# The first product of layer 0's experts as three one-pass products, and its neighbours' loads and tables moved

## The chip, the cores and the metric

The program runs on one core of a Trainium2 chip. Its engines are named as in the profile: PE (TensorE, matmuls), PEld (the weight loads that go with them), DVE (VectorE), ACT (ScalarE), POOL (GpSimd) and SP (SyncE, which here issues DMAs). The metric is the device time of one execution in microseconds (us); lower is better. The kernel before the change takes 3702.06 us, the median of three runs (3697.73 to 3706.18).

## The reference, cut to what matters

Two transformer layers run over 2048 tokens of width 512. Each layer is an attention followed by a mixture of experts. The change is in the mixture of layer 0, which is:

```python
probs = jax.nn.softmax(xr @ Wg, axis=-1)            # 2048 tokens, 8 experts
gate_vals, expert_idx = jax.lax.top_k(probs, 2)
...                                                 # each expert takes at most 640 tokens
dispatched = xr[dispatch_mask.reshape(-1) % S].reshape(E, C, d)      # 8 x 640 x 512
h = jax.nn.relu(jnp.einsum('ecd,edf->ecf', dispatched, w1))          # w1: 8 x 512 x 2048
expert_out = jnp.einsum('ecf,efd->ecd', h, w2)                       # w2: 8 x 2048 x 512
...
out = jnp.einsum('ks,ksm->sm', combine_weights, rerouted)
```

Everything is float32. After it come layer 1's attention, which needs rotation tables (sines and cosines of the positions times two norm vectors) and four weight matrices Wq, Wk, Wv, Wo, and then layer 1's experts.

## The kernel before, in words

Layer 0's attention, layer 0's experts, layer 1's attention and layer 1's experts follow each other. The experts of layer 0 are the class `Experts0` (L1225), called by `layer0_experts` (L1380).

An expert's 640 places are five blocks of 128. The first four are always computed (`FULL` = 4, so 512 places); the fifth is computed only where the expert has tokens there, inside `tc.If(self.used[e])` in `last` (L1318). The inner width 2048 is cut into 16 slices of 128. For each of the 8 x 16 = 128 pairs of expert e and slice k, which are called steps here, `run` (L1352) records:

- `first(e, k)` (L1300): the first product into the PSUM bank `h`. It is four matmuls in `inner` (L1284), one for each 128 of the input width, with a 128x128 piece of w1 as weight and 512 columns of `xT` moving. A float32 matmul stands in the trace as two records. ACT's Relu reads the bank and writes `hT`.
- `second` of the step before (L1309): four matmuls, one for each block, into the banks `o0` to `o3`, which add up over the 16 slices. After the last slice `result` (L1340) scales them by the gate (ACT and DVE in turn) and POOL scatters them with an adding DMA into `x_dram`.
- at each fourth step `last`, the fifth block of a group of four slices (banks `hl` and `ol`), where it is used.
- at the even steps, for the next expert: `fetch` (L1273), POOL's gathering DMA of a block of token rows, and `turn` (L1278), four transposes on PE into the bank `tr` (`transpose4`) and a copy by DVE into `xT`.
- at the steps 4 to 13 of an expert one call of `extra`: first the 16 batches of `rope_tables` (L1170), one per step, then ten loads of 1 MB for layer 1's attention (Wk, Wv, four parts of Wq, four of Wo).

The eight PSUM banks are `h`, `tr`, `o0` to `o3`, `hl`, `ol`, one buffer each. The weights w1 and w2 come in units of two slices by SP's DMAs (`weights0`, L1216), with four and six buffers. PE, DVE, ACT and POOL take their instructions in the order of the recording (`Engines`, L74, keeps it); SP's DMAs and the bodies of the If are placed by the framework's scheduler.

A rotation batch (`batch`, L1185) runs on DVE, ACT (Sin, Abs, Sin), DVE again and then nine small multiplications on POOL, into one buffer `rp_r`, from which SP writes the table to HBM.

After the last expert, `kept.close()` frees the expert weights and `layer1_attention` (L1634) begins: SP loads the token rows `xn` from `x_dram`, and PE starts with the products of the context rows, which need Wk and Wv.

Of the kernel before, what the change touches and what calls it, by code (L numbers as in the profile page):

```python
# [11 lines left out]
F32 = mybir.dt.float32  # L12
BF16 = mybir.dt.bfloat16
I32 = mybir.dt.int32
U32 = mybir.dt.uint32
U16 = mybir.dt.uint16
F32R = mybir.dt.float32r
AF = mybir.ActivationFunctionType
ALU = mybir.AluOpType
# [4 lines left out]
P = 128  # L24
NB = 16
D = 512
NC = D // P
NH = 16
G0 = 8
G1 = 4  # L30
E = 8
SPAN = NB * P
CAP = 640
# [9 lines left out]
FW1 = NC * 2 * FF1  # L43
FW = FW1 + 3 * D
FP8_MAX = 448.0
SCALE = float(np.float32(1.0 / np.sqrt(128.0)))
TWO_PI = float(2.0 * np.pi)
TWO_PI_A = 6.28125
# [34 lines left out]
class Ops:  # L83
# [34 lines left out]
    def t(self, pool, shape, dt, tag, bufs=None):  # L118
        self.uid += 1
        return pool.tile(shape, dt, name=f"{tag}_{self.uid}", tag=tag, bufs=bufs)  # L120
# [59 lines left out]
class Routing:  # L180
# [22 lines left out]
    def turn(self):  # L203
        self.ps = self.r.ops.transpose4(self.psum, self.xn)
# [1011 lines left out]
def weights0(ops, args, pool, e, f):  # L1216

    w1 = ops.t(pool, [P, NC, 256], F32, "w1", KEPT_UNITS["w1"])
    ops.nc.sync.dma_start(out=w1, in_=args["f0_w1"][e, f])
    w2 = ops.t(pool, [P, 2, D], F32, "w2", KEPT_UNITS["w2"])  # L1220
    ops.nc.sync.dma_start(out=w2, in_=args["f0_w2"][e, f])
    return w1, w2


class Experts0:  # L1225
# [7 lines left out]

    SLICES = FF0 // P
    GROUP = 4
    FULL = NBLK0 - 1

    def __init__(  # L1240
        self, ops, tc, args, router, x_dram, sum_dram, small, work, psum, kept_pool, zero, begun
    ):
        self.plain, self.tc = ops.nc, tc
        ops.nc = Engines(tc, ops.nc)
        self.ops, self.args, self.work, self.psum = ops, args, work, psum
        self.kept_pool, self.zero = kept_pool, zero[0:1]
        self.x_dram, self.sum_dram = x_dram, sum_dram
        self.table = router.table
        self.source, self.target = slot_rows(ops, small, self.table[:, :P], P, SPAN // P)

        self.views = dram_disjoint_views(sum_dram, NBLK0)
        self.mark = sum_dram[SUMS - 1 :, :]
        self.xT, self.g, self.h, self.rest, self.outs = {}, {}, {}, {}, {}
        self.w = begun
        self.h_last = ops.t(psum, [P, self.GROUP, P], F32, "hl")
        self.o_last = ops.t(psum, [P, D], F32, "ol")
        ops.nc.vector.memset(self.h_last, 0.0)
        ops.nc.vector.memset(self.o_last, 0.0)

        used = ops.t(small, [P, E], I32, "used")  # L1260
        last = self.table[:, :P].rearrange("p (e b) -> p e b", e=E)[:, :, self.FULL]
        ops.nc.vector.tensor_scalar(used, last, 0.0, None, ALU.is_gt)
        loads, self.used = self.plain.values_load_multi_w_load_instructions(
            used[0:1, :], engines=(mybir.EngineType.PE,), min_val=0, max_val=1,
            skip_runtime_bounds_check_because="it is the result of a comparison",
        )
        for i in loads:
            tc.keep_in_program_order(i)
# [7 lines left out]
        gather(self.ops, g, self.x_dram, self.source[:, col : col + 1])  # L1276

    def turn(self, e, b):  # L1278
        if b == 0:
            self.xT[e] = self.ops.t(self.work, [P, NC, CAP], F32, "xT", 2)  # L1280
        ps = self.ops.transpose4(self.psum, self.g.pop((e, b)))
        self.ops.nc.vector.tensor_copy(self.xT[e][:, :, b * P : (b + 1) * P], ps)

    def inner(self, ps, e, k, s):  # L1284

        w1, at = self.w[e, k // 2][0], k % 2 * P
        for c in range(NC):
            self.ops.nc.tensor.matmul(
                ps, w1[:, c, at : at + P], self.xT[e][:, c, s],
                start=(c == 0), stop=(c == NC - 1),  # L1290
            )

# [5 lines left out]
        )  # L1298

    def first(self, e, k):  # L1300
        n = self.FULL * P
        if k % 2 == 0 and (e, k // 2) not in self.w:
            self.w[e, k // 2] = weights0(self.ops, self.args, self.kept_pool, e, k // 2)
        ps = self.ops.t(self.psum, [P, n], F32, "h")
        self.inner(ps, e, k, slice(0, n))
        hT = self.h[e, k] = self.ops.t(self.work, [P, n], F32, "hT", 4)
        self.ops.nc.scalar.activation(hT, ps, AF.Relu)

    def second(self, e, *slices):  # L1309
        if slices[0] == 0:  # L1310
# [7 lines left out]
    def last(self, e, group, before):  # L1318


        g = self.GROUP
        with self.tc.If(self.used[e]):  # L1322
            if before is not None:
                for i in range(g):
                    self.outer(self.o_last, e, before * g + i, self.rest[e, before][:, i, :])
            if group is not None:
                for i in range(g):
                    s = slice(self.FULL * P, CAP)
                    self.inner(self.h_last[:, i, :], e, group * g + i, s)
        if group is not None:  # L1330
            rest = self.rest[e, group] = self.ops.t(self.work, [P, g, P], F32, "rest", 2)
            self.ops.nc.vector.tensor_scalar(rest, self.h_last, 0.0, None, ALU.max)
        else:
            self.result(e, self.FULL, self.o_last)

            self.ops.nc.sync.dma_start(
                out=self.mark.rearrange("p (a c) -> p a c", a=4), in_=self.zero
            )
# [10 lines left out]
            nc.scalar.activation(y, out, AF.Copy, scale=weight)  # L1349
        scatter_add(self.ops, self.views[b], self.target[:, col : col + 1], y)  # L1350

    def run(self, extra):  # L1352
        for b in range(NBLK0):
            self.fetch(0, b)
            self.turn(0, b)
        groups = self.SLICES // self.GROUP
        steps = [(e, k) for e in range(E) for k in range(self.SLICES)]
        for i, (e, k) in enumerate(steps):
            self.first(e, k)
            if 0 < i < len(steps) - 1:  # L1360
                self.second(*steps[i - 1])
            group, at = divmod(k, self.GROUP)
            if at == self.GROUP - 1:
                self.last(e, group, group - 1 if group else None)
            if e and k == 0:
                self.last(e - 1, None, groups - 1)
            if e + 1 < E and k % 2 == 0:
                b = k // 2 - 2
                if 0 <= b + 2 < NBLK0:
                    self.fetch(e + 1, b + 2)  # L1370
                if 0 <= b < NBLK0:
                    self.turn(e + 1, b)
            if 4 <= k < 14 and extra:
                extra.pop(0)()
        self.second(E - 1, self.SLICES - 2, self.SLICES - 1)
        self.last(E - 1, None, groups - 1)
        self.ops.nc = self.plain


def layer0_experts(ops, tc, args, router, x_dram, sum_dram, small, kept_pool, zero, begun, extra):  # L1380
    with ExitStack() as ctx:
        work = ctx.enter_context(tc.tile_pool(name="b_work", bufs=1))
        psum = ctx.enter_context(tc.tile_pool(name="b_ps", bufs=1, space=PSUM))
        job = Experts0(
            ops, tc, args, router, x_dram, sum_dram, small, work, psum, kept_pool, zero, begun
        )
        job.run(extra(work))

# [466 lines left out]
def xattn_moe_two_layers(ctx: ExitStack, tc: tile.TileContext, args, out):  # L1857
    nc = tc.nc
    const = ctx.enter_context(tc.tile_pool(name="const", bufs=1))
    dram = ctx.enter_context(tc.tile_pool(name="dram", bufs=1, space=DRAM))  # L1860
    ops = Ops(nc, tc, const)
    t = ops.t
# [5 lines left out]
    nw = t(const, [P, 2 * P], F32, "nw")  # L1868
    nc.sync.dma_start(out=nw, in_=args["norms"])
    x0_dram = t(dram, [SPAN, D], F32, "x0_dram")  # L1870
    x1_dram = t(dram, [SPAN, D], F32, "x1_dram")

    x_dram = t(dram, [SUMS, D], F32, "x_dram")
# [10 lines left out]
    begun = {}  # L1884
    zero = []
# [8 lines left out]
    }  # L1894
    layer0_attention(ops, tc, args, x_rows, vec, router0, kept_pool, ahead)

    with tc.tile_pool(name="c_w", bufs=1) as wpool:
        wq = t(wpool, [P, NC, NH * P], F32, "c_wq")
        wk = t(wpool, [P, NC, D], F32, "c_wk")
        wv = t(wpool, [P, NC, D], F32, "c_wv")  # L1900
        wo = t(wpool, [P, NH, D], F32, "c_wo")

        def ahead(work):

            loads = [(wk, args["Wk"]), (wv, args["Wv"])]
            for c in range(4):
                s = slice(c * D, (c + 1) * D)
                loads.append((wq[:, :, s], args["Wq"][:, :, s]))
            for c in range(4):
                h = slice(4 * c, 4 * c + 4)  # L1910
                loads.append((wo[:, h, :], args["Wo"][:, h, :]))
            calls = rope_tables(ops, args, work, nw, rope_dram)

            def load(to, source):

                ops.nc.vector.memset(to[:, 0:1, 0:1], 0.0)
                nc.sync.dma_start(out=to, in_=source)

            return calls + [lambda a=a: load(*a) for a in loads]

        layer0_experts(
            ops, tc, args, router0, x0_dram, x_dram, wpool, kept_pool, zero[0], begun, ahead
        )
        kept.close()
        layer1_attention(
            ops, tc, args, x_rows, (wq, wk, wv, wo), rope_dram, router1, out, wpool
        )
    layer1_experts(ops, tc, args, router1, x1_dram, out)

# [71 lines left out]
```

## Time and profile before

| what | us |
|---|---|
| median of three runs | 3702.06 |
| the profiled execution's own time | 3698.0 |
| its span, first to last instruction | 3696.2 |
| stage of layer 0's attention | 0 to 1277 |
| stage of layer 0's experts | 1277 to 2298 |
| stage of layer 1's attention | 2298 to about 3336 |
| stage of layer 1's experts | to the end |

The stages are read from the first and last starts of the groups. A line of the groups gives line, engine, operation, output tile and input tiles, shapes, count, then busy time, mean duration of one, and the idle time before them with what ended it. L69 is the line of the helper through which every recorded instruction goes, so groups are told apart by their tiles. A matmul's duration in its record has a tail that overlaps the next one; the time between two starts is what a matmul costs in a row of them. A line of the timeline gives start, time, engine, operation, tiles, count, and in brackets the idle time before it.

### The profile page before, as it was taken

The numbers are of one execution on the slowest core, as the hardware profiler recorded it, in microseconds if no ns is written. First come the engines' busy times: TensorE is split into PE (matmuls) and PEld (weight loads), VectorE is DVE, ScalarE is ACT, GpSimd is POOL, SyncE is SP. The second block draws the span as 40 slices with busy tenths as digits, with TensorE's granted clock in tenths as the row PEclk, the third lists the DMA queues.
The fourth block names the chain that finished last, engine by engine and source line by source line (L and its number), as shares of the span: only waits on it lengthen the run. The fifth ranks groups of instructions, "written<-read, shape, count | busy, mean of one in ns | idle before, by whom it ended". The sixth has DMA issues, their size and how long they took to land. (4 is left out here: it accounts for less than half of the span.)

```text
span 3696.2 us, 42676 instructions
## 1 busy us (share of the span) xinstructions
PE 3532.1 (96%) x13220; PEld 2111.1 (57%) x13220; DVE 1756.6 (48%) x4203; ACT 1500.5 (41%) x5601; POOL 1265.6 (34%) x1596
## 2 busy tenths in 40 slices
PE   6899999999999699999999999899999999997998
PEld 3666666788888444444444454455555555554655
DVE  6888899877688521100000000445555555553111
ACT  5777677788877111101100101443444343441111
POOL 6566677654244222101110100423333333321332
PEclk8999999999999799999999999999999999998999
DMA  4556755744523133453332331000001010006333
GB/s 159 167 175 205 260 199 194 275 147 145 177 90 122 52 115 98 135 167 100 105 91 63 104 76 25 31 23 30 27 22 35 22 32 19 21 12 236 69 63 55
DMA packets 156777, 382.80 MB, mean 104 GB/s; under 512 B 18080, under 2 KB 21312, under 8 KB 154752
## 3 DMA queue, kind: packets, MB, share of 16 engines
q1 hardware_dynamic: 138848, 338.49, 27.3%
q0 software_dynamic: 17696, 41.43, 5.9%
q8 instruction: 119, 1.95, 0.2%
q14 instruction: 114, 0.93, 0.1%
HBM read 266.32 MB, written 113.52 MB: 103 GB/s over the span
## 5 line engine op out<-in xcount | busy, mean ns | idle before, releaser
L69 PE MATMUL h<-xT,w 128*128 128x512 f32 x1024 | 467.2, 594 | 4.0 <-PEq L1322 1.1
L69 PE MATMUL o<-w,hT 128*128 128x512 f32 x1024 | 460.8, 592 | 0.0
L69 ACT ACTIVATE hT<-h 128x512 f32<-128x512 f32 x128 | 76.3, 596 | 852.8 <-PE h L69 852.8
L69 PEld LDWEIGHTS o<-w,hT 128*128 128x128 f32 x1024 | 194.2, 190 | 243.7 <-issue 243.0
L69 DVE COPY xT<-tr 128x512 f32<-128x512 f32 x79 | 54.4, 688 | 572.4 <-PE tr L69 572.4
L69 PEld LDWEIGHTS h<-xT,w 128*128 128x128 f32 x1024 | 189.6, 190 | 231.0 <-issue 229.3
L69 ACT ACTIVATE p<-sc,sm_nm 128x128 f32<-128x128 f32 (+1 forms) x768 | 302.7, 420 | 20.9 <-PE tr L69 10.4
L69 PE MATMUL mm<-w,xq 128*128 128x512 f32 x1024 | 275.8, 411 | 5.5 <-DVE xq L69 4.0
L69 PE MATMUL sc<-kT,qT 128*128 128x128 f32 (+1 forms) x1536 | 267.4, 310 | 4.7 <-ACT qT L69 4.4
L69 ACT ACTIVATE hn_sq<-mm 128x128 f32<-128x128 f32 x768 | 214.8, 280 | 128.1 <-PE mm L69 105.4
L69 POOL DMA_INDIRECT x_dram<-y,e_target x40 | 62.6, 1564 | 572.0 <-ACT y L69 562.3
L69 PE MATMUL pv<-pT,v 128*128 128x256 f32 (+1 forms) x768 | 255.8, 456 | 1.4 <-ACT pT L69 1.4
L69 PEld LDWEIGHTS sc<-kT,qT 128*128 128x128 f32 x1536 | 222.4, 191 | 46.0 <-issue 29.7
L69 PE MATMUL mm<-c_wq,hT 128*128 128x512 f32 x512 | 231.4, 595 | 0.7 <-DVE qn L69 0.7
L69 PE MATMUL po<-c_wo,oT 128*128 128x512 f32 x512 | 231.4, 595 | 0.0
L69 DVE TENSOR_REDUCE sm_nm<-sc 128x4 f32<-128x512 f32 (+1 forms) x256 | 175.5, 685 | 92.1 <-PE sc L69 92.0
L69 PE MATMUL po<-w,cq 128*128 128x512 f32 x512 | 192.4, 457 | 24.8 <-DVE cq L69 3.4
L69 POOL TENSOR_TENSOR hn_rs<-hn_rs,mhalf 128x4 f32<-128x4 f32 x192 | 205.2, 1069 | 16.0
L69 PEld LDWEIGHTS mm<-w,xq 128*128 128x128 f32 x1024 | 185.4, 191 | 43.6 <-DVE xq L69 4.8
L69 ACT ACTIVATE rms_sq<-mm 128x128 f32<-128x128 f32 x384 | 106.8, 278 | 251.5 <-PE mm L69 230.8
L69 PE MATMUL h<-e_w,xT 128*128 (+1 forms) x624 | 200.5, 465 | 4.3 <-DMA e_w<-in_f_w 3.5
L69 PE MATMUL mm<-w,xk 128*128 128x512 f32 x512 | 187.3, 508 | 0.9 <-POOL w L69 0.8
(248 smaller groups left out, 6388.6 us busy)
## 6 DMA issues: line engine op xcount, KB each, us to landing
w<-in_f_w SPq DMA_DIRECT2D x128, 512.0 KB, 3.7
kept_w<-st SPq DMA_DIRECT2D x66, 512.0 KB, 2.9
w<-kept_w SPq DMA_DIRECT2D x66, 512.0 KB, 5.6
x_dram<-xr SPq DMA_DIRECT2D x64, 256.0 KB, 2.0
xr<-x_dram SPq DMA_DIRECT2D x64, 256.0 KB, 2.8
e_w<-in_f_w SPq DMA_DIRECT2D x8, 1408.0 KB
xk<-in_ctxT SPq DMA_DIRECT2D x32, 256.0 KB, 3.8
xv<-in_ctxT SPq DMA_DIRECT2D x32, 256.0 KB, 3.0
```

The lines of the kernel that those rows point to most:

```text
L69: return self.tc.keep_in_program_order(call(*args, **kwargs))
```

## The change

The first product of the four full blocks is no longer a float32 matmul. Both operands are cut into an upper part `hi`, whose lowest 12 bits are zero, and the exact rest. With w = hi + lo for the weights and x likewise, and S = `SPLIT` = 4096, three matmuls of type float32r are made for each 128 of the input width: hi_w by hi_x and lo_w by S lo_x, added in the bank `h`, and (hi_w - S lo_w) by (hi_x - S lo_x) in the bank `tr`. The result is (1 + 1/S) times the first sum less 1/S times the second.

- `cut`, `split` (new): three DVE instructions and one ACT instruction of 128x512 make the three parts of a slice of w1, one step ahead of their use, with two buffers for each part.
- `turn`: ACT copies the transposed block out of `tr`, then DVE (three instructions) and ACT (two more) make the parts of x. The fifth block is kept whole (`x_last`), copied by DVE.
- `first`: 12 one-pass matmuls in place of 4 float32 ones; then ACT scales the second bank (`less`), DVE combines it with the first (`hT`), and ACT's Relu works in place in SBUF.
- `extra` is called at the even steps from 4 on (4, 6, ... 14): 16 rotation batches, then the loads of Wk and Wv, so that they end in the third expert.
- The space for the parts of x is taken from where Wq and Wo lay. Wq is loaded at step 2 of the last expert, when the pool `b_even` is closed; Wo after the last expert, when the pool of expert weights is closed, in four DMAs of 1 MB that stand ahead of layer 1's first loads of token rows in SP's order.

The second product, the fifth block and all that comes before and after are unchanged.

```diff
     def turn(self, e, b):
...
+        ps = self.ops.transpose4(self.psum, self.g.pop((e, b)))
+        if b == self.FULL:
+            x = self.x_last[e] = t(work, [P, NC, P], F32, "x_last", 2)
+            nc.vector.tensor_copy(x, ps)
+            return
...
+        upper, lower, part = (x[:, :, b * P : (b + 1) * P] for x in self.x[e])
+        raw = t(work, [P, NC, P], F32, "x_raw", 2)
+        nc.scalar.copy(raw, ps)
+        hi = self.cut(raw, [P, NC, P], "x_hi")
+        nc.scalar.copy(upper, hi)
+        nc.vector.tensor_tensor(raw, raw, hi, ALU.subtract)
+        nc.scalar.activation(lower, raw, AF.Copy, scale=SPLIT)
+        nc.vector.scalar_tensor_tensor(part, raw, -SPLIT, hi, ALU.mult, ALU.add)
+
+    def cut(self, raw, shape, tag):
+
+        hi = self.ops.t(self.work, shape, F32, tag, 2)
+        self.ops.nc.vector.tensor_scalar(
+            hi.bitcast(U32), raw.bitcast(U32), 12, 12, ALU.logical_shift_right,
+            ALU.logical_shift_left,
+        )
+        return hi
+
+    def split(self, e, k):
...
+        hi = self.cut(raw, [P, NC, P], "w_hi")
+        nc.scalar.copy(upper, hi)
+        nc.vector.tensor_tensor(lower, raw, hi, ALU.subtract)
+        nc.vector.scalar_tensor_tensor(part, lower.bitcast(F32), -SPLIT, hi, ALU.mult, ALU.add)
+        self.split_w[e, k] = upper, lower, part
...
     def first(self, e, k):
-        ps = self.ops.t(self.psum, [P, n], F32, "h")
-        self.inner(ps, e, k, slice(0, n))
-        hT = self.h[e, k] = self.ops.t(self.work, [P, n], F32, "hT", 4)
-        self.ops.nc.scalar.activation(hT, ps, AF.Relu)
+        upper, lower, part = self.split_w.pop((e, k))
+        x_upper, x_lower, x_part = self.x[e]
+        rest = t(self.psum, [P, n], F32, "h")
+        for i, (w, x) in enumerate(((upper, x_upper), (lower, x_lower))):
+            for c in range(NC):
+                nc.tensor.matmul(
+                    rest, w[:, c, :], x[:, c, :],
+                    start=(i == 0 and c == 0), stop=(i == 1 and c == NC - 1),
+                )
+
+        parts = t(self.psum, [P, n], F32, "tr")
+        for c in range(NC):
+            nc.tensor.matmul(
+                parts, part[:, c, :], x_part[:, c, :], start=(c == 0), stop=(c == NC - 1)
+            )
+        hT = self.h[e, k] = t(self.work, [P, n], F32, "hT", 4)
+        less = t(self.work, [P, n], F32, "less", 2)
+        nc.scalar.activation(less, parts, AF.Copy, scale=-1.0 / SPLIT)
+        nc.vector.scalar_tensor_tensor(hT, rest, 1.0 + 1.0 / SPLIT, less, ALU.mult, ALU.add)
+        nc.scalar.activation(hT, hT, AF.Relu)
...
         for i, (e, k) in enumerate(steps):
+            if i + 1 < len(steps):
+                self.split(*steps[i + 1])
             self.first(e, k)
...
-            if 4 <= k < 14 and extra:
+            if k >= 4 and k % 2 == 0 and extra:
                 extra.pop(0)()
+            if (e, k) == (E - 1, 2):
+                late()
```

More of the change, by code (lines that the diff above doesn't have):

```diff
@@ L45 @@
 FP8_MAX = 448.0
+SPLIT = 4096.0
 SCALE = float(np.float32(1.0 / np.sqrt(128.0)))
@@ L1240, in __init__ @@
     def __init__(
-        self, ops, tc, args, router, x_dram, sum_dram, small, work, psum, kept_pool, zero, begun
+        self, ops, tc, args, router, x_dram, sum_dram, small, work, psum, kept_pool, zero, begun,
+        even_pool,
     ):
@@ L1245, in __init__ @@
         self.ops, self.args, self.work, self.psum = ops, args, work, psum
-        self.kept_pool, self.zero = kept_pool, zero[0:1]
+        self.kept_pool, self.zero, self.even_pool = kept_pool, zero[0:1], even_pool
         self.x_dram, self.sum_dram = x_dram, sum_dram
@@ L1252, in __init__ @@
         self.mark = sum_dram[SUMS - 1 :, :]
-        self.xT, self.g, self.h, self.rest, self.outs = {}, {}, {}, {}, {}
+        self.x, self.x_last, self.g, self.h, self.rest, self.outs = {}, {}, {}, {}, {}, {}
+        self.split_w = {}
         self.w = begun
@@ L1278, in turn, with inner @@
     def turn(self, e, b):
-        if b == 0:
[L1280 to L1284, printed above, removed]
+        nc, t, work = self.ops.nc, self.ops.t, self.work
+        ps = self.ops.transpose4(self.psum, self.g.pop((e, b)))
[3 more added lines that the diff above has]
+            return
+        if b == 0:
+            pool = work if e % 2 else self.even_pool
+            self.x[e] = [t(pool, [P, NC, self.FULL * P], F32R, f"x{i}") for i in range(3)]
+        upper, lower, part = (x[:, :, b * P : (b + 1) * P] for x in self.x[e])
[14 more added lines that the diff above has]
+    def split(self, e, k):
+        nc, t = self.ops.nc, self.ops.t
+        if k % 2 == 0 and (e, k // 2) not in self.w:
+            self.w[e, k // 2] = weights0(self.ops, self.args, self.kept_pool, e, k // 2)
+        raw = self.w[e, k // 2][0][:, :, k % 2 * P : (k % 2 + 1) * P]
+        upper, lower, part = (
+            t(self.work, [P, NC, P], F32R, f"w{i}", 2) for i in range(3)
+        )
[4 more added lines that the diff above has]
+        self.split_w[e, k] = upper, lower, part
+    def inner(self, ps, e, k):
         w1, at = self.w[e, k // 2][0], k % 2 * P
@@ L1288, in inner @@
             self.ops.nc.tensor.matmul(
-                ps, w1[:, c, at : at + P], self.xT[e][:, c, s],
+                ps, w1[:, c, at : at + P], self.x_last[e][:, c, :],
                 start=(c == 0), stop=(c == NC - 1),
@@ L1300, in first @@
     def first(self, e, k):
-        n = self.FULL * P
-        if k % 2 == 0 and (e, k // 2) not in self.w:
-            self.w[e, k // 2] = weights0(self.ops, self.args, self.kept_pool, e, k // 2)
-        ps = self.ops.t(self.psum, [P, n], F32, "h")
-        self.inner(ps, e, k, slice(0, n))
-        hT = self.h[e, k] = self.ops.t(self.work, [P, n], F32, "hT", 4)
-        self.ops.nc.scalar.activation(hT, ps, AF.Relu)
+        nc, t, n = self.ops.nc, self.ops.t, self.FULL * P
+        upper, lower, part = self.split_w.pop((e, k))
[11 more added lines that the diff above has]
+                parts, part[:, c, :], x_part[:, c, :], start=(c == 0), stop=(c == NC - 1)
+            )
+        hT = self.h[e, k] = t(self.work, [P, n], F32, "hT", 4)
[3 more added lines that the diff above has]
+        nc.scalar.activation(hT, hT, AF.Relu)
     def second(self, e, *slices):
@@ L1327, in last @@
                 for i in range(g):
-                    s = slice(self.FULL * P, CAP)
-                    self.inner(self.h_last[:, i, :], e, group * g + i, s)
+                    self.inner(self.h_last[:, i, :], e, group * g + i)
         if group is not None:
@@ L1350, in result, with run @@
         scatter_add(self.ops, self.views[b], self.target[:, col : col + 1], y)
-    def run(self, extra):
+    def run(self, extra, late):
+        self.split(0, 0)
         for b in range(NBLK0):
@@ L1377, in run, with layer0_experts, last_expert @@
         self.ops.nc = self.plain
-def layer0_experts(ops, tc, args, router, x_dram, sum_dram, small, kept_pool, zero, begun, extra):
-    with ExitStack() as ctx:
-        work = ctx.enter_context(tc.tile_pool(name="b_work", bufs=1))
+def layer0_experts(
+    ops, tc, args, router, x_dram, sum_dram, small, kept_pool, zero, begun, extra, late
+):
+    with ExitStack() as ctx, ExitStack() as even:
+        even_pool = even.enter_context(tc.tile_pool(name="b_even", bufs=1))
+        work = ctx.enter_context(tc.tile_pool(name="b_work", bufs=1, side="right"))
         psum = ctx.enter_context(tc.tile_pool(name="b_ps", bufs=1, space=PSUM))
         job = Experts0(
-            ops, tc, args, router, x_dram, sum_dram, small, work, psum, kept_pool, zero, begun
-        )
-        job.run(extra(work))
+            ops, tc, args, router, x_dram, sum_dram, small, work, psum, kept_pool, zero, begun,
+            even_pool,
+        )
+        def last_expert():
+            even.close()
+            late()
+        job.run(extra(even_pool), last_expert)
 ORDER1 = (
@@ L1895, in xattn_moe_two_layers, with load @@
     layer0_attention(ops, tc, args, x_rows, vec, router0, kept_pool, ahead)
-    with tc.tile_pool(name="c_w", bufs=1) as wpool:
-        wq = t(wpool, [P, NC, NH * P], F32, "c_wq")
+    with ExitStack() as attention1:
+        wpool = attention1.enter_context(tc.tile_pool(name="c_w", bufs=1))
         wk = t(wpool, [P, NC, D], F32, "c_wk")
         wv = t(wpool, [P, NC, D], F32, "c_wv")
-        wo = t(wpool, [P, NH, D], F32, "c_wo")
+        late = []
+        def load(to, source):
+            ops.nc.vector.memset(to[:, 0:1, 0:1], 0.0)
+            nc.sync.dma_start(out=to, in_=source)
@@ L1903, in ahead @@
         def ahead(work):
-            loads = [(wk, args["Wk"]), (wv, args["Wv"])]
-            for c in range(4):
[L1907 to L1917, printed above, removed]
@@ L1919, in ahead, with large @@
-            return calls + [lambda a=a: load(*a) for a in loads]
+            calls = rope_tables(ops, args, work, nw, rope_dram)
+            return calls + [lambda: load(wk, args["Wk"]), lambda: load(wv, args["Wv"])]
+        def large(name, shape, count, source):
+            pool = attention1.enter_context(tc.tile_pool(name=name, bufs=1))
+            w = t(pool, shape, F32, name)
+            for c in range(4):
+                s = slice(c * count, (c + 1) * count)
+                part = (slice(None), slice(None), s) if name == "c_wq" else (slice(None), s)
+                nc.sync.dma_start(out=w[part], in_=source[part])
+            late.append(w)
@@ L1921, in xattn_moe_two_layers @@
         layer0_experts(
-            ops, tc, args, router0, x0_dram, x_dram, wpool, kept_pool, zero[0], begun, ahead
+            ops, tc, args, router0, x0_dram, x_dram, wpool, kept_pool, zero[0], begun, ahead,
+            lambda: large("c_wq", [P, NC, NH * P], D, args["Wq"]),
         )
         kept.close()
+        large("c_wo", [P, NH, D], 4, args["Wo"])
         layer1_attention(
-            ops, tc, args, x_rows, (wq, wk, wv, wo), rope_dram, router1, out, wpool
+            ops, tc, args, x_rows, (late[0], wk, wv, late[1]), rope_dram, router1, out, wpool
```

## The prediction

> **What bounds the kernel now.** I read the busy time by stage first, then the groups, then the timeline. In the stage of layer 0's experts:
>
> ```profile
> core 0: us, PE busy (x) PEld busy (x) DVE busy (x) ACT busy (x) POOL busy (x), PEclk, DMA share, GB/s
> 1277.00:2298.00 1021.00, 1014.29 (x2831) 483.59 (x2830) 100.76 (x286) 105.66 (x201) 132.67 (x215) 1.00 0.34 97
> ```
>
> PE is busy for 1014 of 1021 us at full clock; DVE and ACT work for a tenth of it. So PE's work is the stage's time, and work put on DVE and ACT is free as long as PE never waits for it. Whose work that is, from the groups:
>
> ```profile
> L69 PE MATMUL h<-xT,w 128*128 128x512 f32 x1024 | 467.2, 594 | 4.0 <-PEq L1322 1.1
> L69 PE MATMUL o<-w,hT 128*128 128x512 f32 x1024 | 460.8, 592 | 0.0
> L69 ACT ACTIVATE hT<-h 128x512 f32<-128x512 f32 x128 | 76.3, 596 | 852.8 <-PE h L69 852.8
> L69 DVE COPY xT<-tr 128x512 f32<-128x512 f32 x79 | 54.4, 688 | 572.4 <-PE tr L69 572.4
> L69 PE MATMUL mm<-w,xq 128*128 128x512 f32 x1024 | 275.8, 411 | 5.5 <-DVE xq L69 4.0
> ```
>
> The first product (`h`) and the second (`o`) share the stage. Only `h` changes. What one costs is the time between starts:
>
> ```profile
> 1801.48 3.60 PE L69 MATMUL h<-xT,w 128*128 128x512 f32 x8
> 1804.91 3.60 PE L69 MATMUL o<-w,hT 128*128 128x512 f32 x8
> 1805.17 0.60 ACT L69 ACTIVATE hT<-h 128x512 f32<-128x512 f32 x1 [6.27 <-PE h L69]
> ```
>
> `o` starts 3.43 us after `h`: 8 records of 0.429. A step is 6.86 us, 128 steps 878 us; the rest is the fifth block and transposes. ACT starts 0.26 us after the stream ended.
>
> **The gain.** The price of a one-pass float32r record is in layer 0's attention, where `mm<-w,xq` is such a product (64 block passes x 2 x 8 matmuls = 1024 records, one each):
>
> ```profile
> 690.72 0.60 PE L69 MATMUL tr<-ident,kn 128*128 128x128 f32 x4
> 691.08 2.12 PE L69 MATMUL mm<-w,xq 128*128 128x512 f32 x8
> 693.04 0.59 PE L69 MATMUL pv<-pT,v 128*128 128x256 f32 x2
> ```
>
> The last transpose starts at 691.05 and costs 0.109; so eight records run from 691.16 to 693.04, 0.235 each. Over the whole stage the quartiles of the time between starts are 231 and 237 ns, the lowest 229. Twelve are 2.82 us, so a step loses 3.43 - 2.82 = 0.617 us: **128 x 0.617 = 79.0 us off PE** (75 at 237 ns, 88 at 229).
>
> **Plain steps keep it.** DVE gets per step a cut (`st<-raw`, the same operation, median 0.418), a subtraction (`ra<-ra,rb`, 0.692), and two fused multiply-adds (`xr<-po,pscale,xr`, 0.744): 2.6 us of 6.25. ACT gets a copy (0.62, as `w<-st`), a scaling and a Relu (0.60 to 0.63): 1.9. The new wait: bank `h` is now freed by DVE's add, not by ACT's Relu. Counted from the end of `first(k)` on PE: `less` 0.27 to 0.87, add to 1.65. PE has 3.43 us of `second(k-1)` before it wants `h` again, and the parts of slice k+1 were made a step before. Hidden. Where a block is turned, DVE has 1.85 more for x, and ACT 1.9; the same bookkeeping as below puts the next add at about 9.2, PE's need at 10.1. Hidden, with 0.9 to spare.
>
> **Rotation steps don't.** DVE's order in the changed program is: parts of w for k+1, add of k, parts of x, rotation batch, parts of w for k+2, add of k+1. The x parts wait for transposes behind `second(k-1)`, and everything behind them waits too. The prices of a batch:
>
> ```profile
> 1322.09 0.60 PE L69 MATMUL tr<-ident,g 128*128 128x128 f32 x4
> 1322.72 0.69 DVE L69 COPY xT<-tr 128x512 f32<-128x512 f32 x1 [38.07 <-PE tr L69]
> 1323.33 0.41 DVE L69 TENSOR_SCALAR rp_a<-inv,posf 128x64 f32<-128x64 f32 x2
> 1326.63 0.48 DVE L69 TENSOR_SCALAR rp_a<-inv,posf 128x64 f32<-128x64 f32 x2
> 1326.73 1.81 POOL L69 TENSOR_TENSOR rp_r<-rp_o,nw 128x64 f32<-128x64 f32 x6 [47.89 <-ACT rp_o L69]
> 1328.51 0.92 POOL L69 TENSOR_TENSOR rp_r<-rp_o,qw 128x64 f32<-128x64 f32 x3
> ```
>
> A copy out of `tr` starts 0.63 after the transposes, a batch holds DVE for 3.30 (1323.33 to 1326.63, ACT's part within it), POOL's nine follow for 2.7. With zero at the end of `first(k)`: transposes at 3.43, x in SBUF at 3.43 + 0.63 + 0.59 = 4.65, three DVE steps to 6.65, batch to 9.95, parts of w to 11.85, add to 12.6. POOL works beside these last four; in the trace a batch's first step took 0.48 beside POOL and 0.41 alone, so I add 15%, 0.3: 12.9. PE wants `h` at 3.43 + 0.44 + 2.82 + 3.43 = 10.1. It **stalls 2.8 us** (2.3 to 3.3). This hits k = 4, 6, 8, 10 of the experts with 16 batches at six each, 0, 1 and 2: 12 x 2.8 = 33.6. At k = 12 the turned block is the fifth (one copy, no parts): 0.9, twice, 1.8. At k = 14 nothing is turned, and the batch starts at 1.65: hidden. SP's write of each table stands behind weight loads that wait for earlier steps only, so `rp_r` is free in time.
>
> **The clock.** PE idle in part of one window of 3.4 us has cost the clock of the next, but not always:
>
> ```profile
> 1233.60:1237.00 3.40, 1.73 (x11) 1.55 (x12) 2.12 (x10) 0.52 (x3) 0.00 (x0) 1.00 0.20 77
> 1237.00:1240.40 3.40, 1.69 (x7) 1.03 (x6) 3.09 (x16) 0.59 (x1) 0.00 (x0) 0.50 0.00 0
> 2319.00:2322.40 3.40, 1.69 (x4) 0.38 (x3) 1.39 (x2) 0.59 (x1) 2.59 (x3) 1.00 0.18 53
> 2322.40:2325.80 3.40, 0.85 (x6) 0.64 (x7) 2.51 (x6) 0.59 (x1) 0.67 (x2) 1.00 0.06 24
> ```
>
> After 1.73 us busy of 3.40 the granted clock fell to 0.50; after 1.69 it did not yet. I take a half-busy window as the edge. A stall of 2.8 leaves a window under half when over 1.7 of it fall into one: with windows at any offset, about 2 of 3 times, 8 of 12. A halved window loses 1.7 us of PE's work; what falls into `second` only shortens the next stall, what falls into `first` counts, about 1.5. **8 x 1.5 = 12 us** (0 to 17).
>
> **The ends.** Start: a block of x takes ACT and DVE 2.4 us (copy, cut, subtraction, scaling) where a copy took 1.9; with the last one's parts the first product starts 1.7 later. `first(0, 1)` waits for an add behind `less`: 0.9 more than for a Relu. At the end the last Relu comes 1.1 later. Wo's 4.2 MB stand before `xn` on SP: at 330 GB/s (1610 to 1620 us) 12.7 us, so `xn` lands at about 2322.6; DVE took it up at 2323.2, behind other work. The cover has 0.6 us to spare: 0.5 (0 to 3). Sum 4.2. Wq in the last expert, Wk and Wv run beside PE, with weights loaded four units ahead; nothing is queued that PE needs within 25 us. No cost.
>
> **Sum**: -79.0 + 33.6 + 1.8 + 12.0 + 4.2 = -27.4. The profiled execution took 3698.0; it becomes 3670.6. It stood 4.1 below the median of the runs shown, so I predict **3675** as a median.
>
> **Rivals.**
> - *Stalls without clock loss*: 3675 - 12 = **3663**. For: one half-busy window passed unpunished, and DVE's lag never leaves PE idle for a whole window. Against: the window at 1233.6. The Trainium skill, "TensorE: Matmul & The Clock Gate", section "HAM oscillation — how this bites in real kernels", speaks for it: it asks for no idle gap over about 3.4 us, and mine are shorter. The trace disagrees at 1238.26, where a gap of 2.80 us sat before the fall.
> - *No stalls*: DVE is ready in time, so only pace and ends count: 3675 - 12 - 33.6 - 1.8 = **3628**. It needs 2.8 us less in the chain; for it speaks that DVE's work per two steps (10.5 us) is below PE's 12.9. Against: its order, and 2 us in which it waits for x.
> - *POOL holds DVE*: a DVE instruction beside POOL waits for a whole POOL instruction (0.31) each time: four, 1.2 per stall, 17 in all, and two more clock losses: **3695**. For: `z<-q_c,q_m` has a median of 0.693 and a longest of 1.39, beside long POOL work. Against: the batch beside POOL lost 15%. The Trainium skill, "SBUF — State Buffer", section "SBUF: two separate sides", calls the port pair shared by the two an exclusive lock for a whole instruction; by it this case would hold, and the 1.39 agrees.
> - *Slower*: the one-pass record doesn't run at 0.235 here. The page's own row is 275.8 / 1024 = 0.269 for a record; if that is the price in `first`, twelve are 3.23, the gain 26, and the sum +25.5: **3728**. It decides from 0.252, where gain and 51.6 of losses meet. For: weights change at every record, and a record lasts hardly longer than its weight load (0.188). Against: 0.235 has the same load, and the 0.269 holds gaps between groups. At two records a product, as float32 has, it would be worse still; the count of 1024 rules that out.
>
> **How the numbers follow.** Forecast 0.57 (its own range 3648 to 3692: pace -8.6 to +3.7, stalls -6 to +6, clock -12 to +5, Wo up to +2.5), no clock loss 0.17, no stalls 0.09, POOL 0.09, slower 0.08. The range of 3636 to 3697 leaves out the no-stall and the slower case, 0.17; its low end is half the stalls, no clock loss and 229 ns (3675 - 12 - 17.7 - 8.6). A measurement here can tell 0.2%, 7.4 us: faster is under 3694.7. Forecast, first two rivals and a part of the third give 0.86; the rest of the third 0.06; slower 0.08.
>
> **What would show it.** `h` and `tr` products with starts 0.235 apart, 2.82 from first `h` to first `o`; PE idle before `h`, ended by DVE's `hT`, 12 times near 2.8 between 1300 and 1590, and nowhere near that in experts 3 to 7, where steps take 6.25; PEclk at 0.5 for some windows there; DVE at some 45% of the stage. Steps above 6.3 in experts 3 to 7 would break the gain's term, absent idle the stalls' term.

## The result and the profile after

The changed kernel takes 3664.98 us (median of four runs, 3664.19 to 3666.24) against 3702.22 for the kernel before: a ratio of 0.990, 95% interval 0.9888 to 0.9912. The forecast was 3675, with a range of 3636 to 3697. The profiled execution took 3665.4, span 3663.6; the one of before 3698.0 and 3696.2.

The groups of the changed kernel, from its page (busy time, mean ns of one, idle time before them and what ended it):

```profile
L70 PE MATMUL o<-w,hT 128*128 128x512 f32 x1024 | 463.7, 592 | 3.3 <-PEq L1379 1.6
L70 PE MATMUL h<-x,w 128*128 128x512 f32 x1024 | 300.9, 436 | 29.9 <-DVE hT L70 28.5
L70 DVE SCALAR_TENSOR_TENSOR hT<-h,less 128x512 f32<-128x512 f32 x128 | 88.2, 689 | 393.7 <-ACT less L70 393.7
L70 ACT ACTIVATE less<-tr 128x512 f32<-128x512 f32 x128 | 76.2, 595 | 404.4 <-PE tr L70 404.4
```

One number matters here: PE stood idle for 28.5 us before `h`, and what ended it was DVE's `hT`, the add that frees the bank. Before the change all idle time ahead of `h` was 4.0. The busy times by engine of the stage, from its first matmuls to its end (columns: window and us, then PE, PEld, DVE, ACT, POOL busy with counts, granted clock, DMA share, GB/s):

```profile
1277.00:2263.00 986.00, 949.25 (x3347) 588.58 (x3348) 439.25 (x851) 311.27 (x547) 169.45 (x216) 0.97 0.34 97
```

DVE is busy for 439 of 986 us (45%), PE's clock is at 0.97 and no longer at 1.00. A step without a batch, on PE:

```profile
1810.24 2.41 PE L70 MATMUL h<-x,w 128*128 128x512 f32 x8
1812.48 1.08 PE L70 MATMUL tr<-x,w 128*128 128x512 f32 x4
1813.40 3.59 PE L70 MATMUL o<-w,hT 128*128 128x512 f32 x8
1816.43 0.80 PE L70 MATMUL h<-x,w 128*128 128x512 f32 x1
```

From `h` to `h` it is 6.19 us where it was 6.87. The four records into `tr` start 0.92 before `o`: 0.229 each.

A step of expert 0 with a batch, in order of time (the turned block's transposes end at 1324.8):

```profile
1320.93 3.59 PE L70 MATMUL o<-w,hT 128*128 128x512 f32 x8
...
1321.82 0.69 DVE L70 SCALAR_TENSOR_TENSOR hT<-h,less 128x512 f32<-128x512 f32 x1 [10.05 <-ACT less L70]
...
1325.62 0.43 DVE L70 TENSOR_SCALAR x_hi<-x_raw 128x512 uint32<-128x512 uint32 x1 [3.11 <-ACT x_raw L70]
...
1327.42 0.41 DVE L70 TENSOR_SCALAR rp_a<-inv,posf 128x64 f32<-128x64 f32 x2
...
1327.57 3.59 PE L70 MATMUL o<-w,hT 128*128 128x512 f32 x8
...
1330.71 0.42 DVE L70 TENSOR_SCALAR w_hi<-w 128x512 uint32<-128x512 uint32 x1
1330.82 3.04 POOL L70 TENSOR_TENSOR rp_r<-rp_o,nw 128x64 f32<-128x64 f32 x6 [46.57 <-ACT rp_o L70]
1331.17 0.69 DVE L70 TENSOR_TENSOR w<-w,w_hi 128x512 fp32r<-128x512 f32 x1
1331.22 0.62 ACT L70 CAST w<-w_hi 128x512 fp32r<-128x512 f32 x1 [0.49 <-DVE w_hi L70]
1331.75 0.59 ACT L70 ACTIVATE less<-tr 128x512 f32<-128x512 f32 x1
1331.97 0.69 DVE L70 SCALAR_TENSOR_TENSOR w<-w,w_hi 128x512 fp32r<-128x512 f32 x1
1332.58 0.68 DVE L70 SCALAR_TENSOR_TENSOR hT<-h,less 128x512 f32<-128x512 f32 x1
...
1333.32 3.48 PE L70 MATMUL h<-x,w 128*128 128x512 f32 x8 [2.15 <-DVE hT L70]
```

Read it down DVE: it waits 3.11 us for the transposes, then parts of x, the batch from 1327.42, the parts of w from 1330.71, and only then the add at 1332.58. Its input `less` has been ready since 1332.3; that is late too, because on ACT `less` stands behind the copy of `w_hi`, which waits for DVE. PE's `o` at 1327.57 takes 3.43, so PE wants the bank at 1331.00; it starts at 1333.32 (the row names 2.15 idle before it, since records have a tail). The stall is 2.3 us here and 2.4 in the later ones.

What such a stall does to the clock, by windows of 3.41 us (columns as above):

```profile
1330.29:1333.70 3.41, 1.26 (x5) 0.38 (x4) 3.25 (x9) 1.83 (x4) 2.88 (x6) 1.00 0.00 0
1333.70:1337.12 3.42, 3.42 (x10) 2.68 (x9) 1.39 (x2) 0.73 (x2) 2.95 (x5) 0.50 0.20 73
1337.12:1340.53 3.41, 3.41 (x11) 1.84 (x10) 0.69 (x1) 1.23 (x2) 0.00 (x0) 1.00 0.85 277
```

The stall leaves PE 1.26 busy in one window; in the next it works all the time at half the clock and loses 1.7 us.

To compare kernels without the noise of the unchanged stages, the experiments use the time from PE's first transposes of `g` to its first `mm<-c_wk` (**the stage**): 1268.93 to 2298.36, 1029.4 us, before, and 1272.99 to 2266.66, 993.7, after. That is 35.8 less. The profiled executions as a whole differ by only 32.6, mainly because layer 0's attention, which is the same in both, took 3.9 us longer in this one.

### The profile page after: what moved, and what is told of

Read it like the earlier page. It is cut to its first block, busy times and chain, and to the rows that moved or that the text cites. A ratio compares the mean times of both kernels' runs of the same rounds, so it can differ in the third digit from the quotient of the medians.

```text
span 3663.6 us, 44828 instructions
## 1 busy us (share of the span) xinstructions
PE 3469.3 (95%) x13732; PEld 2217.8 (61%) x13732; DVE 2095.4 (57%) x4771; ACT 1708.2 (47%) x5953; POOL 1302.5 (36%) x1596
## 5 line engine op out<-in xcount | busy, mean ns | idle before, releaser
L70 PE MATMUL h<-x,w 128*128 128x512 f32 x1024 | 300.9, 436 | 29.9 <-DVE hT L70 28.5
L70 DVE SCALAR_TENSOR_TENSOR hT<-h,less 128x512 f32<-128x512 f32 x128 | 88.2, 689 | 393.7 <-ACT less L70 393.7
L70 ACT ACTIVATE less<-tr 128x512 f32<-128x512 f32 x128 | 76.2, 595 | 404.4 <-PE tr L70 404.4
L70 PEld LDWEIGHTS h<-x,w 128*128 128x128 f32 x1024 | 193.2, 194 | 115.0 <-DVE hT L70 40.6
```

The lines of the kernel that those rows point to most:

```text
L70: return self.tc.keep_in_program_order(call(*args, **kwargs))
```

## The experiments

The theory: the loss beside the gain comes from the place of a batch in DVE's order, behind the parts of x and ahead of the add that frees the bank. Rivals: it comes from the amount of work on DVE in those two steps; or from POOL holding DVE up.

### The batches at the slices where no block is turned

```diff
-            if k >= 4 and k % 2 == 0 and extra:
+            if k >= 5 and k % 2 == 1 and extra:
                 extra.pop(0)()
```

> The rotation batches stand at the odd slices from 5 on, where no block is turned; nothing else differs from the changed kernel. My theory (DVE's order: parts of x and a batch ahead of the add that frees bank h): a batch then begins right behind the add of its own step, about 1.5 us after the end of that step's first product, and lasts 3.3; the parts of w follow to about 6.9, the next add has ended by about 7.8, PE wants h at 9.6. No stall is left: the changed kernel shows twelve stalls of about 2.4 with a halved clock window (1.7) behind each, and two of 0.9, together 51 us, so 3665 - 51 = 3614, PE idle before h near 0 after the first step and the clock at full in experts 0 to 2. Rival 1 (it is the amount of work that DVE has in those two steps, wherever it stands): the stalls stay, 3655 to 3665. Rival 2 (the batch's POOL part holds DVE up): a quarter to a half of the loss stays, 3630 to 3640.

Measured: 3617.48 us, ratio to before 0.977 (0.9751 to 0.9783); the stage is 943.2, 50.5 less than in the changed kernel. The stage's busy times and the group of `h` in this kernel:

```profile
1277.00:2211.00 934.00, 924.53 (x3342) 577.31 (x3343) 436.32 (x850) 310.75 (x546) 156.85 (x215) 1.00 0.36 102
```

```profile
L70 PE MATMUL h<-x,w 128*128 128x512 f32 x1024 | 292.7, 428 | 2.8 <-DVE hT L70 1.4 <-ACT x L70 0.2
```

DVE does the same 436 us of work, and PE's wait for `hT` falls from 28.5 to 1.4, the clock is back at 1.00. The amount of work is not the cause. Of the 51 us predicted, the stage shows 50.5 (the medians of the runs differ by 47.5).

### The batch ahead of the turned block

```diff
+            if k >= 4 and k % 2 == 0 and extra:
+                extra.pop(0)()
             if e + 1 < E and k % 2 == 0:
                 b = k // 2 - 2
...
-            if k >= 4 and k % 2 == 0 and extra:
-                extra.pop(0)()
```

> The batch stays at the even slices, but is recorded ahead of the turned block: DVE then has parts of w, add, batch, parts of x, parts of w, add. My theory: the batch fills the time in which DVE waits for the transposes, so that x parts end about 7.0 us after the end of the first product, parts of w about 8.9, the add about 9.6, and PE wants h at 10.0: no stall, or a few tenths, 3614 to 3620. Rival 1 (amount of work in the two steps): nothing changes, 3655 to 3665. Rival 2 (POOL holds DVE): POOL's nine now run beside the parts of x and w, stalls of 1 us stay, about 3630.

Measured: 3616.78 us (ratio 0.977, 0.9752 to 0.9785). The group of `h` in this kernel:

```profile
L70 PE MATMUL h<-x,w 128*128 128x512 f32 x1024 | 291.4, 426 | 2.8 <-DVE hT L70 1.4 <-ACT x L70 0.2
```

The stage is 947.4, 4.2 above the run before. Of these, 1.3 lie ahead of the second step, and 2.6 are the "few tenths": in four steps of experts 0 and 1 in which the fifth block is computed, PE waits for the fifth block's Relu, which DVE does behind the add, and each of these steps takes 0.6 to 0.75 more. The batch now runs while DVE would wait for the transposes. Same engine, same step, same instructions, another order: and the steps from the second to the last take 910.7 us where the changed kernel's take 958.1. POOL's nine multiplications run beside the parts of x and w here as well, and no stall of a microsecond comes back, so POOL does not hold DVE up.

### The batches at every slice

```diff
-            if k >= 4 and k % 2 == 0 and extra:
+            if 4 <= k < 14 and extra:
                 extra.pop(0)()
```

> The batches at every slice from 4 to 13, as in the kernel before, the rest as changed: this undoes the spacing alone. My theory: a batch at an odd slice is hidden and a batch at an even slice stalls PE as it does now, so what counts is how many even slices have a batch and a turned block: four in expert 0 and three in expert 1 (7 in place of 12), and one of 0.9: 7 x 4.1 + 0.9 = 30 us in place of 51, so about 3644. Rival 1 (amount of work): two batches in two steps bring DVE's work to 13.7 us beside PE's 12.8, worse than one batch in two steps: each of the eight pairs of slices would cost more than now, about 6 each, 3665 or above.

Measured: 3648.18 us (ratio 0.986, 0.9838 to 0.9871), 3644 expected. So the spacing to every second slice, taken alone, costs 17 us net: it puts every batch onto a slice where a block is turned. The four expected stalls in expert 0 and the three in expert 1 are there: the pairs of steps take 4.0 to 4.8 us more than undisturbed ones (4.1 expected); slice 15 of expert 0 waits once more, 1.9. That the time comes so near is partly luck. Only five of the seven stalls halved a window. And batches one slice apart meet in their one buffer `rp_r`: DVE waited five times, 8.5 us in all, for SP's write of the table before (`DMA rope<-rp_r`), which it never does in the changed kernel. In the two pairs without a halved window PE waited a second time, 0.7 and 1.2 us ahead of the next transposes, so they lost about as much as the others. Two stalls of this kernel, the window with the stall and the one behind it:

```profile
1387.77:1391.18 3.41, 1.20 (x3) 0.19 (x1) 2.80 (x8) 1.87 (x5) 2.23 (x5) 1.00 0.00 0
1391.18:1394.59 3.41, 3.20 (x6) 1.88 (x7) 2.78 (x10) 0.94 (x3) 1.41 (x6) 0.50 0.28 115
1370.71:1374.12 3.41, 1.44 (x4) 0.37 (x2) 2.73 (x8) 1.93 (x5) 2.16 (x4) 1.00 0.00 0
1374.12:1377.53 3.41, 3.13 (x13) 2.55 (x14) 2.54 (x10) 1.14 (x3) 1.49 (x6) 1.00 0.29 114
```

With 1.20 busy in the window the clock fell behind it, with 1.44 it did not. The last 0.3 us of the second stall lie in the window behind.

### Stalls of chosen lengths

The kernel of the first experiment, and behind the turned block at slices 4, 6, 8 and 10 of experts 3 to 6:

```diff
+                if k in (4, 6, 8, 10):
+                    for _ in range({3: 3, 4: 4, 5: 5, 6: 6}.get(e, 0)):
+                        self.ops.nc.vector.tensor_tensor(
+                            self.idle[1], self.idle[0], self.idle[0], ALU.subtract
+                        )
```

> On the kernel with the batches at the odd slices, DVE gets extra subtractions of 128x512 (results not used) behind the turned block at slices 4, 6, 8 and 10: three of them in expert 3, four in expert 4, five in expert 5, six in expert 6. My theory: DVE has 0.9 us to spare there (a batch of 3.3 gave stalls of 2.4), one subtraction holds it for about 0.7, so the stalls are near 1.2, 1.9, 2.6 and 3.3, four of each, 36 us. A window of 3.41 us in which PE stood idle for 2.1 or more cost the next window half its clock in all runs so far, one with under 1.6 never: so 1.2 and 1.9 cost no clock, 2.6 and 3.3 do when the stall lies in one window, 4 to 8 of 8, 1.7 each. Sum 43 to 50, one time of 3660 to 3667. If the clock went by the stall alone, all sixteen would cost it: 63, 3680. If stalls cost no clock: 36, 3653. If DVE's amount of work in the two slices counts and not the place, stalls do not grow by the length of each added subtraction.

Measured: one time of 3666.41 us; the stage is 51 longer than without. The stalls, from the lengths of the two steps beside 12.79 of an undisturbed pair, were 1.2, 1.9, 2.6 and 3.4: each subtraction added the 0.7 that it holds DVE. Nothing but work in DVE's queue was added here, so this shows most directly that a stall is as long as that queue runs late. Stalls followed by a halved window: 0 of 4, 1 of 4 (I had expected none at 1.9), 3 of 4 and 4 of 4; two of the last four halved two windows on end. Nor did "under 1.6 never" hold: in the changed kernel a window with 1.41 us of idle, at 1207 us, was followed by a halved one. The one that expert 5 was spared, and its next:

```profile
1916.58:1919.99 3.41, 1.64 (x7) 1.38 (x8) 3.17 (x6) 2.05 (x4) 0.00 (x0) 1.00 0.01 2
1919.99:1923.40 3.41, 3.41 (x13) 1.98 (x12) 0.85 (x2) 1.19 (x2) 0.00 (x0) 1.00 0.50 159
1930.24:1933.65 3.41, 1.18 (x3) 0.19 (x1) 3.24 (x6) 1.11 (x2) 0.00 (x0) 1.00 0.00 0
1933.65:1937.06 3.41, 3.27 (x6) 1.95 (x7) 2.40 (x5) 1.25 (x2) 0.00 (x0) 0.50 0.00 0
```

The first stall is spread over two windows (1.64 busy in one) and costs no clock; the next, 15.44 us or four and a half windows later, lies within one.

### The add ahead of the parts of w

```diff
-            if i + 1 < len(steps):
-                self.split(*steps[i + 1])
             self.first(e, k)
+            if i + 1 < len(steps):
+                self.split(*steps[i + 1])
```

> As the changed kernel, but the parts of w for the next slice are recorded behind the first product and its add, not ahead of them; the batch stays behind the turned block at the even slices. My theory: with zero at the end of the first product, the batch ends at 9.7 as now, the next add then follows at once, 9.7 to 10.4, where PE wants h at 10.0; but the next slice's parts of w come behind it, and the first of them is there only at 10.4 + 0.4 + 0.6 = 11.4. The stall shrinks from 2.4 to about 1.4 and no window is idle for 2.1 us, so no clock is lost: 12 x 1.4 = 17 in place of 49, about 3632. In plain slices the parts still come in time. Rival (amount of work): nothing changes, 3655 to 3665.

Measured: 3666.36 us (ratio 0.990, 0.9887 to 0.9917), no better than the changed kernel. My figure of 3632 was wrong. A stalled step of this kernel, ACT, DVE and PE:

```profile
1472.43 3.59 PE L70 MATMUL o<-w,hT 128*128 128x512 f32 x8
...
1475.36 0.31 ACT L70 ACTIVATE rp_o<-rp_n 128x128 f32<-128x128 f32 x1 [0.29 <-DVE rp_n L70]
...
1475.58 0.58 ACT L70 ACTIVATE less<-tr 128x512 f32<-128x512 f32 x1
...
1476.19 0.69 DVE L70 SCALAR_TENSOR_TENSOR hT<-h,less 128x512 f32<-128x512 f32 x1 [0.46 <-ACT less L70]
1476.80 0.44 DVE L70 TENSOR_SCALAR w_hi<-w 128x512 uint32<-128x512 uint32 x1
1476.91 0.63 ACT L70 ACTIVATE hT<-hT 128x512 f32<-128x512 f32 x1 [0.76 <-DVE hT L70]
...
1477.45 0.60 ACT L70 CAST w<-w_hi 128x512 fp32r<-128x512 f32 x1
...
1478.10 3.36 PE L70 MATMUL h<-x,w 128*128 128x512 f32 x8 [2.08 <-ACT w L70]
```

The releaser of PE is no longer DVE's `hT` but ACT's `w`. I had left ACT's own order out: `less` stands behind the batch's last Sin (to 1475.67), so the add came 0.7 later than I put it, and the first part of w stands behind the Relu, 0.2 more; with the 1.4 that I had, this makes 2.2. PE wanted to start at 1475.86 and did at 1478.10: 2.2, where the changed kernel has 2.3 to 2.4. One wait was exchanged for another. All but the first of its stalls left PE idle for 2.0 to 2.1 in a window and halved the next one.

### The first product as before, with the neighbours moved

`first`, `turn` and `inner` as before, without `split`; the spacing of the batches and the moved loads as changed.

> The first product as it was (float32, Relu by ACT, the block copied by DVE), with the rotation batches at every second slice and the loads of Wq, Wk, Wv and Wo moved as in the change. My theory: DVE has little to do, PE never waits, and the moved loads are not waited for: 3702, within 4 us. The difference to the run with the batches at odd slices is then what the three one-pass products bring by themselves: 128 x 0.69 = 88 us by the steps without a stall. If Wo's load ahead of the token rows costs, the first product of layer 1 on xn starts up to 3 us later behind the first on the context rows than the 28.8 us of the kernel before.

Measured: 3706.15 us (ratio 1.0013, 1.0003 to 1.0022), 4 us above the 3702 I gave, at the edge of my margin. The stage is 1028.7 against 1029.4 before, so neither spacing nor loads cost anything there: with a free DVE a batch is hidden at the turned slices too. Set beside the first experiment, **the three one-pass products, with the work that makes their parts, bring 1028.7 - 943.2 = 85.5 us**. The extra time lies ahead of the stage:

```profile
1263.57 0.65 PE L70 MATMUL mm<-r_two,r_one 128*128 128x384 f32 x1
...
1264.37 2.20 SPq L1938 DMA_DIRECT2D c_wo<-in_Wo  x4
...
1274.47 1.09 PE L70 MATMUL tr<-ident,g 128*128 128x128 f32 x4 [10.25 <-DMA g<-x_dram,e_source]
```

In this kernel the scheduler sent Wo's loads out beside the first gathers, and the first transposes came 10.9 us after the router's last matmul; in the kernel before it was 7.0, in the changed one 7.15. So I held Wo back, with a small DVE write into each part, recorded at the end of the last expert.

> As the run with the first product as it was and the neighbours moved, but Wo's load waits for a small DVE write recorded behind the last expert, so that it goes out after the last expert as in the changed kernel. In the run before, the scheduler sent Wo's 4.2 MB out at 1264 us, together with the first gathers of layer 0's experts, whose landing then took 8.8 us and not 3.3. If these 4 us are what that run lost against the kernel before, this one is at 3702, within 2, and PE's first transposes start 7.0 us after the router's last matmul, as in the kernel before, not 10.9. If the moved batches or loads of Wq, Wk and Wv cost, the 4 us stay.

Measured: 3705.35 us (ratio 1.0010, 1.0001 to 1.0019): not the 3702 I gave. The stage stays at 1028.3 and the transposes came 6.9 after the router, as expected, but layer 1's first product on `xn` now starts 34.5 us behind its first on the context rows, 28.8 before. SP's queue in this kernel, first the two early parts of Wo:

```profile
2304.93 0.85 SPq L1942 DMA_DIRECT2D c_wo<-in_Wo  x2
2319.40 0.61 SPq L1342 DMA_DIRECT2D x_dram<-e_zero  x1
2320.10 0.87 SPq L1942 DMA_DIRECT2D c_wo<-in_Wo  x2
2321.02 1.08 SPq L1465 DMA_DIRECT2D xn<-x_dram  x2
```

and in the changed kernel:

```profile
2274.60 0.61 SPq L1392 DMA_DIRECT2D x_dram<-e_zero  x1
2275.30 2.09 SPq L1991 DMA_DIRECT2D c_wo<-in_Wo  x4
2277.43 1.45 SPq L1516 DMA_DIRECT2D xn<-x_dram  x3
```

Here two of Wo's parts went out while the last outputs were still being scattered. The mark `e_zero`, which waits for those, came 14.4 us after the first `mm<-c_wk` (2305.02), where it came 8 after it in the changed kernel (2266.66), and the token rows behind it came later by as much. The five scatters took 10.5 us to land in this kernel (median from issue), against 5.1 to 5.7 in the kernel before, the changed one and the run above, where no part of Wo was on its way beside them. That Wo's 2 MB slowed them fits these numbers and the order; no run varies it alone. In the changed kernel Wo stands behind the mark and costs nothing: the first product on `xn` came 28.15 after the first on the context rows, and DVE took `xn` up directly behind its own earlier work.

## Why the prediction was right, and where its sizes were off

- **The gain**: predicted 79.0 us, 0.617 a step. Plain steps fell from 6.87 to 6.17 to 6.19, so 0.68 to 0.70 a step, 88 for 128. The mis-sized term is the price of a record: 0.229 here (a step of 6.18 less 3.43 for `o`, over twelve) against the 0.235 taken from layer 0's attention; the prediction's low end of 229 ns is the mean here. What makes the attention's records 6 ns longer stays open: beside a busy DVE their median is 235 ns and without it 234, and beside POOL it is 235 either way.
- **Plain and turned steps hide the new work**: right. In experts 3 to 7 PE does not wait for `hT`; the 0.9 us to spare in a turned step are borne out by the sweep (three subtractions, 2.1 us, gave stalls of 1.2).
- **The stalls**: right in place and number: twelve at k = 4, 6, 8, 10 of experts 0 to 2, two of 0.9 behind k = 12 of experts 0 and 1. Their size was 2.3 to 2.4, not 2.8: x in SBUF 4.7 after the end of `first(k)` (4.65 predicted), x parts to 6.5 (6.65), batch to 9.8 (9.95), w parts to 11.65 (11.85), add to 12.3 (12.9). The largest piece is the 0.3 I added for POOL; another is my sum for the parts of x, which made 2.0 of three prices that add up to 1.85. 28 us in place of 33.6.
- **The clock**: 12 us predicted, 8 windows of 1.5; there were twelve, and each cost the full 1.7, 20.5 us. The failed step is "with windows at any offset, about 2 of 3 times". It does not follow from its own edge: a stall of 2.8 at any offset leaves over 1.7 in one window of 3.41 about 8 times in 10 (it fails only for 0.6 of the 3.41 us of offsets). Nor is there a sharp edge at half a window. In the profiles of all nine kernels, from 100 us on and with busy time counted as in the views of windows, 81 windows at full clock in which PE stood idle for 2.1 us or more were each followed by a halved one, and of 8892 with under 1.5 idle, 1 was; between, 36 of 59 were. A stall of 2.4 has 2.2 of idle in its rows; to leave 2.1 in one window it must lie almost whole within it, which at any offset would be some 4 times in 10. But the stalls are not at any offset. With the edges of the windows taken from where the granted clock changes, the twelve idle stretches of the changed kernel began 0.0 to 0.9 us into a window, so each ended within it. A stalled pair of steps takes 16.88 us with a halved window, 4.95 windows (about 24.0 us and 7.0 windows where the fifth block is computed), so the next stall falls into nearly the same place in its window; without a halved window the pair takes 15.2, 4.45 windows, and the next is moved by half a window. The sweep showed one such move. That this is why all twelve were hit is argued, not shown.
- **The ends**: 1.8 more for the turned first blocks (1.7 predicted), 0.6 for `first(0, 1)` (0.9), 1.3 at the end (1.1), nothing for Wo (0.5; the rate put in for it, 330 GB/s, is 323 in the window that the prediction names).
- **The sum**: -88 + 28 + 1.8 + 20.5 + 3.7 = -34 in place of my -27.4; the stage shows -35.8, and the last 1.8 I cannot place. The gain was 9 larger and the stalls 5.6 smaller, against 8.5 more for the clock; that these errors cancel in part is luck. The profiled execution came out 5.2 below the 3670.6 of the sum, though layer 0's attention took 3.9 more in it; the rest of the 10 us to the forecast is the 4.1 added for the median, which this kernel's median (3665.0) does not show over its profiled execution (3665.4).
- **The rivals**: 3665 lies within 2 us of the rival "stalls without clock loss" (3663), but that one is wrong: twelve windows were halved. A time alone would have chosen it. The Trainium skill, "TensorE: Matmul & The Clock Gate", section "HAM oscillation — how this bites in real kernels", asks for no idle gap over about 3.4 us; here 2.2 us of idle in one window sufficed twelve times. The gap of 2.80 that the prediction set against this rival ran from 1235.46 to 1238.26, and the clock had fallen at 1237.0, so only 1.5 of it sat before the fall. "POOL holds DVE" is wrong as well, though the two do meet: POOL's first six multiplications took 3.04 beside DVE's parts of w (row at 1330.82), 1.81 before the change, while DVE's rows there stayed at 0.42, 0.69 and 0.69 (a cut a little later, at 1333.18, took 0.50). The Trainium skill's page "SBUF — State Buffer", section "SBUF: two separate sides", describes an exclusive lock on a port pair that the two share. Here nearly all the added time stood in POOL's rows; that the lock is its cause is not shown. "No stalls" (3628) is what the kernel becomes when the batch is moved: 3617. "Slower" fell with the price of a record.

## What to carry to other kernels

Work that "fits", because an engine is idle for half of its time, is free only if nothing the bottleneck waits for stands behind it in that engine's order: 3.3 us of DVE work cost 4.1 us of PE time behind a wait for transposes, and next to nothing one slice later or one place earlier. When a bank's release moves from one engine to another, write out that engine's queue between two releases, and then the queue of each engine that feeds it; moving one link only, as in the fifth experiment, hands the wait to the next one. Price a stall of PE with the clock it may cost in the next window, and check a predicted time term by term, because errors cancel.

## What the runs showed that I had not expected

- The spacing of the batches to every second slice, a part of the change, cost 17 us net beside the old spacing (3665 against 3648), because it lined them up with the turned blocks; the old spacing has a cost of its own, DVE's waits for `rp_r`. Moved by one slice, the same spacing gives 3617, 2.3% below the kernel before and 1.3% below the changed one.
- Wo's 4.2 MB cost nothing behind the mark, but cost about 4 us beside the first gathers and about 6 in the kernel where half of it went out ahead of the mark.
